# Two placements changed in a two-layer graph transformer kernel: a tile's projection copied two tiles later, and the missing-edge mask made during the experts

## The chip, the cores and the metric

The kernel runs on one core of a Trainium2 chip. A core has five engines that run side by side, each with a queue of its own: TensorE (PE, matmuls and transpositions), VectorE (DVE), ScalarE (ACT), GpSimd (POOL) and SyncE (SP, which here only starts transfers). The metric is the device time of one execution in microseconds (us). Results in matmuls stand in PSUM banks until DVE or ACT copies them to SBUF.

## What is computed

625 nodes with 512 features go through two layers. Each adds to `x` a graph network and a linear attention over the normalized rows, and then a mixture of experts. Cut to what the change touches:

```python
edge_index = jnp.stack([src, dst])
xn = layernorm(x)
x = x + rgcn(xn, edge_index, edge_type) + linear_attention(xn)   # layer 0
x = x + experts_0(layernorm(x))          # one of 8 experts for a row
xn = layernorm(x)
x = x + gat_network(xn, edge_index) + linear_attention_1(xn)     # layer 1
x = x + experts_1(layernorm(x))          # router on x @ Wg

def gat_conv(x, edge_index, W, b, a_src, a_dst, n):
    src, dst = edge_index, with a loop added for each node
    h = x @ W
    s_src, s_dst = h @ a_src, h @ a_dst
    e = leaky_relu(s_src[src] + s_dst[dst], 0.2)
    coef = softmax of e over the edges of each dst
    return segment_sum(h[src] * coef, dst) + b
# gat_network, first step: x1 = gat_conv(x, ..., W1, ...) + x @ Wsk1 + bsk1
```

The kernel does the graph attention densely: with a 625 x 625 matrix of edge counts and a mask that is -1e30 where a pair has no edge.

## The kernel before

The nodes are five tiles of 125 rows (P = 125, NT = 5). Matrices of counts (`cnt0`, `cnt1`, one for each kind of edge of layer 0) are 125 x 5 x 625 in float32 and stay in SBUF throughout.

Most of the order of instructions is the framework's: it sorts the instructions of each engine by their place in the program, their priority and what they wait for. Where `manual_schedule` is entered, the named engines take the written order instead. PE's order is written out in the whole of the part described here.

**End of layer 0's network.** The loop at L651 to L668 goes through the tiles: matmuls for the tile's own weights and for both relations, then on DVE `x += ps` (L659) and the layer norm (`layernorm`, L104 to L113); the tile before is transposed on PE in between (L125). The relations' weight matrices are mixed by DVE just before, in 58 long operations (L330). Behind this loop in the program come small constants of the expert stage: `up`, an index row that POOL's iota makes (L599) and DVE casts (L601), and `last_row` (L673, L675).

**The mask.** Then, for each tile (L712 to L716), POOL adds `cnt1` to `cnt0` (L713) and a loop to each node (L714), and DVE writes the mask over `cnt1` (L715). POOL's and DVE's queues are not written out by hand here. The result, `cnt` and `neg`, is first read by the first graph attention (L965, L973).

**The experts (L729 to L924).** DVE works out for each row a place in a sorted buffer (`slot`, L785). POOL scatters the normalized rows to that buffer in HBM by five indirect transfers (L810); SP reads them back expert by expert (`gathered`, L820). `block(i)` multiplies the rows of one expert by its first matrix, and its activation is done on ACT (L862) and DVE (L864); `rest()` multiplies by the second and writes the result out. The loop over i = 1 to 9 runs block i ahead of the rest of block i-1. Experts 0 and 1 take their rows from SBUF by a one-hot product, not from the buffer. `sf` (L893) is the place as a float, from which the last block's rows are selected. At the end POOL gathers each tile's results (`yg`, L917), and the last block's share arrives by matmuls (`held`).

**The projection stage (L1032 to L1071).** For each tile: `scaled` adds the experts' results to `x` on DVE (L1033), once for `held` and once for `yg`; `arrived` takes statistics (L1038, L1040 on DVE, the root on ACT at L1042); `normal` finishes them (L1047, L1048 on DVE) and writes the normalized row on ACT (L1049); the tile is transposed on PE (L125) and copied to `xnT` by `evac` (L72 on ACT); and four matrix products (eight matmuls in the trace) project it to 258 columns (L138): 128 of `h`, two scores, and 128 of the skip. ACT copies `h` with the scores (L1054), DVE adds the bias to the skip (L1055). The orders of PE, DVE and ACT are all written by hand. In turn t of the loop: arrival of t+1, normalization of t, transposition of t and its copy, then projection of t-1 and its two copies. Behind the stage `key(0)` projects for the linear attention, and the first graph attention begins with the row of scores (L943).

`evac` (L69 to L74) alternates between ACT and DVE by a counter, or takes ACT alone while `scalar_only` is set; the counter counts in both cases. It serves the transpositions of the attention passes, of `y1T`, and of the last router (`routed` at L1261 to L1277) later on.

PSUM has one-bank buffers in a pool of four (`ps1`, from which `one_bank()` takes) and two-bank buffers in another.

Of the kernel before, what the change touches and what calls it, by code (L numbers as in the profile page):

```python
# [8 lines left out]
F32 = mybir.dt.float32  # L9
# [4 lines left out]
OP = mybir.AluOpType  # L14
# [4 lines left out]
P = 125  # L19
NT = 5  # L20
D = 512
KD = 4
# [10 lines left out]
NEG_BIG = -1.0e30  # L33


def cols(t):
    return slice(t * P, (t + 1) * P)


def ks(k):  # L40
    return slice(k * 128, (k + 1) * 128)
# [3 lines left out]
def kernel(ctx: ExitStack, tc: tile.TileContext, A, out: bass.AP):  # L45
    nc = tc.nc
# [8 lines left out]
    xn = xv[:, :, :D]  # L55
    xnT = const.tile([128, KD, N], F32, name="xnT")
    cnt0 = const.tile([P, NT, N], F32, name="cnt0")
    cnt1 = const.tile([P, NT, N], F32, name="cnt1")
    ident = const.tile([128, 128], F32, name="ident")
# [7 lines left out]
    scalar_only = [True]  # L67

    def evac(dst, src):  # L69
        turn[0] += 1  # L70
        if scalar_only[0] or turn[0] % 2:
            nc.scalar.copy(dst, src)  # L72
        else:
            nc.vector.tensor_copy(dst, src)  # L74
# [45 lines left out]
    def transpose_rows(psum, src, dst, t, k0=0):  # L120

        n = src.shape[1] // 128
        pt = psum.tile([128, n, 128], F32, name="ps1")
        for k in range(n):
            nc.tensor.transpose(pt[:, k, :P], src[:, ks(k)], ident[:P, :P])  # L125
        evac(dst[:, k0:k0 + n, cols(t)], pt[:, :, :P])
# [9 lines left out]
    def mm(ps, pairs):  # L136
        for i, (l, r) in enumerate(pairs):
            nc.tensor.matmul(ps, l, r, start=(i == 0), stop=(i == len(pairs) - 1))  # L138
# [28 lines left out]
    def two_banks():  # L167
        return banks[0].tile([128, 2 * BANK], F32, name="ps2")

    def one_bank():  # L170
        return banks[1].tile([128, BANK], F32, name="ps1")
# [229 lines left out]
    for n in BGROUPS:  # L401
        k = BROWS * n
# [3 lines left out]
        ps = one_bank()  # L406
# [70 lines left out]
    ps1 = ctx.enter_context(tc.tile_pool(name="ps1", bufs=4, space=PSUM))  # L477
# [80 lines left out]
    sums = []  # L558
    for t in range(NT):
        ps = one_bank()  # L560
# [90 lines left out]
    for t in range(NT):  # L651
        ps = begun[t] if t in begun else one_bank()
# [17 lines left out]
    lpool2 = ctx.enter_context(tc.tile_pool(name="late2", bufs=1, side="right"))  # L670
# [18 lines left out]
    def softmax8(pool, ps, bias=None):  # L689
        lg = pool.tile([P, NT, 8], F32, name="lg")  # L690
        if bias is None:
            nc.vector.tensor_copy(lg, ps)
        else:
            nc.vector.tensor_add(lg, ps, bias)
        mx = pool.tile([P, NT], F32, name="mx")
        nc.vector.tensor_reduce(mx, lg, AX.X, OP.max)
        nc.vector.tensor_sub(lg, lg, mx[:, :, None].to_broadcast([P, NT, 8]))
        nc.scalar.activation(lg, lg, AF.Exp)
        sm = pool.tile([P, NT], F32, name="sm")
        nc.vector.tensor_reduce(sm, lg, AX.X, OP.add)  # L700
        nc.vector.reciprocal(sm, sm)
        nc.vector.tensor_mul(lg, lg, sm[:, :, None].to_broadcast([P, NT, 8]))
        return lg

    def router(pool, wr, bias=None):
# [2 lines left out]
            mm(ps[:P, 8 * t:8 * t + 8], [(xnT[:, k, cols(t)], wr[:, 8 * k:8 * k + 8]) for k in range(KD)])  # L708
        return softmax8(pool, ps[:P, :8 * NT].rearrange("p (t e) -> p t e", e=8), bias)


    for t in range(NT):  # L712
        nc.gpsimd.tensor_add(cnt0[:, t, :], cnt0[:, t, :], cnt1[:, t, :])  # L713
        nc.gpsimd.tensor_add(cnt0[:, t, cols(t)], cnt0[:, t, cols(t)], ident[:P, :P])  # L714
        nc.vector.tensor_scalar(cnt1[:, t, :], cnt0[:, t, :], 0.0, NEG_BIG, op0=OP.is_equal, op1=OP.mult)  # L715
    cnt, neg = cnt0, cnt1  # L716

    junk_pool = []

# [9 lines left out]
    with ExitStack() as st:  # L729
# [7 lines left out]
        ps = one_bank()  # L737
# [46 lines left out]
        slot = rows.tile([P, NT], I32, name="slot")  # L784
# [95 lines left out]
        def scores():  # L880
            w = w8.tile([128, KD, 258], F32, tag="w", name="wl1")
            junk_pool.append(rows)
            for i, n in ((0, "L1_gnn_W1"), (130, "L1_gnn_Wsk1")):
                nc.sync.dma_start(w[:, :, i:i + 128], A[n].rearrange("(k p) m -> p k m", p=128))
            for k in range(KD):
                for i in range(2):
                    weight_dot(w[:, k, 128 + i:129 + i], w[:, k, :128], a1[i])
            wl1.append(w)

        def last_rows():  # L890

            sf = rows.tile([P, NT], F32, name="sf")
            nc.vector.tensor_add(sf, lo, hi)  # L893
            ps = two_banks().rearrange("p (t q) -> p t q", q=128)
            for t in range(NT):
                nc.tensor.transpose(ps[:, t, :P], sf[:, t:t + 1].to_broadcast([P, 128]), ident[:P, :P])
            sel = hp.tile([128, NT, 128], F32, tag="sel", name="sel_last", bufs=NEAR)[:, :, :P]
            nc.vector.tensor_scalar(sel, ps[:, :NT, :P], last_row, None, op0=OP.is_equal)
            return sel

        rest = block(0)
        for i in range(1, 8 + SURE):
            if i == 4:
                sel_last = last_rows()
            if i == 7 + SURE:
                scores()
            after = block(i)
            rest()
            rest = after
# [21 lines left out]
    with ExitStack() as st:  # L931
# [94 lines left out]
        with ExitStack() as s1:  # L1026
# [5 lines left out]
            def scaled(t, m):  # L1032
                nc.vector.scalar_tensor_tensor(x[:, t, :], m, top[:, t:t + 1], x[:, t, :], op0=OP.mult, op1=OP.add)  # L1033

            def arrived(t):
                scaled(t, yg[t])
                st6 = small.tile([P, 6], F32, name="ln_st")
                nc.vector.bn_stats(st6, x[:, t, :])  # L1038
                mv = small.tile([P, 2], F32, name="ln_mv")
                nc.vector.bn_aggr(mv, st6)  # L1040
                sd = small.tile([P, 1], F32, name="ln_sd")
                nc.scalar.activation(sd, mv[:, 1:2], AF.Sqrt, bias=eps5[:P])  # L1042
                return mv, sd

            def normal(t, mv, sd):
                rs = small.tile([P, 2], F32, name="ln_rs2")
                nc.vector.reciprocal(rs[:, 0:1], sd)  # L1047
                nc.vector.tensor_scalar(rs[:, 1:2], mv[:, 0:1], rs[:, 0:1], -1.0, op0=OP.mult, op1=OP.mult)  # L1048
                nc.scalar.activation(xn[:, t, :], x[:, t, :], AF.Identity, scale=rs[:, 0:1], bias=rs[:, 1:2])  # L1049

            def projected(t):
                ps = one_bank()
                mm(ps[:P, :258], [(xnT[:, k, cols(t)], wl1[:, k, :]) for k in range(KD)])
                nc.scalar.copy(h1[:, t, :], ps[:P, :130])  # L1054
                nc.vector.tensor_add(sk1[:, t, :], ps[:P, 130:258], bb1)  # L1055

            scalar_only[0] = True
            with tc.manual_schedule(engines={mybir.EngineType.DVE, mybir.EngineType.Activation}):
                for t in range(NT):
                    scaled(t, held[t])  # L1060
                ahead = arrived(0)
                for t in range(NT):
                    this = ahead
                    if t < NT - 1:
                        ahead = arrived(t + 1)
                    normal(t, *this)
                    transpose_rows(ps1, xn[:, t, :], xnT, t)
                    if t:
                        projected(t - 1)
                projected(NT - 1)  # L1070
            scalar_only[0] = False  # L1071
            gather_pool.close()
            hp = s1.enter_context(tc.tile_pool(name="heads", bufs=2))
            key(0)
# [3 lines left out]
            for t in range(NT):  # L1078
                ps = one_bank()
                mm(ps[:P, :128], [(att.cT[:, j, cols(t)], h1[:, j, :128]) for j in range(NT)])  # L1080
                nc.vector.scalar_tensor_tensor(y1[:, t, :], ps[:P, :128], att.rd[:, t:t + 1], sk1[:, t, :],
                                               op0=OP.mult, op1=OP.add)
# [33 lines left out]
            behind = None  # L1116
            for h in range(16):
# [10 lines left out]
                behind = h, hm  # L1128
# [5 lines left out]
        with ExitStack() as s2:  # L1134
# [13 lines left out]
            with tc.tile_pool(name="rows2", bufs=1) as rp:  # L1148
# [5 lines left out]
                ps = one_bank()  # L1154
# [5 lines left out]
                ps = one_bank()  # L1160
# [23 lines left out]
                ps = two_banks()  # L1184
# [80 lines left out]
            for t in range(NT):  # L1265
                ps = one_bank()
                mm(ps[:P], [(att.cT[:, j, cols(t)], h3[:, j, :]) for j in range(NT)])
                nc.vector.scalar_tensor_tensor(sk3[:, t, :], ps[:P], att.rd[:, t:t + 1], sk3[:, t, :],
                                               op0=OP.mult, op1=OP.add)
# [10 lines left out]
    with ExitStack() as st:  # L1280
# [44 lines left out]
        ps = one_bank()  # L1325
# [4 lines left out]
        for i in range(2):  # L1330
            for lo, hi in ((0, 3), (3, NT)):
                ps = one_bank().rearrange("p (t q) -> p t q", q=128)
# [13 lines left out]
        ahead = [one_bank(), one_bank()]  # L1346
        for t in range(2):
            summed(ahead[t], t, range(7))
        for t in range(NT):
            if t < 2:  # L1350
                ps = ahead[t]
                summed(ps, t, [7])
            else:
                ps = one_bank()
# [48 lines left out]
```

## Time and profile before

| | us |
|---|---|
| runs, and their median | 1008.1, 1011.93, 1012.15; median 1011.93 |
| the profiled execution | 1008.68 |
| its span | 1006.9 |
| PE busy in the span | 926.3 |
| DVE busy | 513.6 |
| ACT busy | 246.9 |
| POOL busy | 155.6 |

The granted TensorE clock is 0.967 of full speed on average over the span. A busy engine counts only instructions of arithmetic; a time in the profile begins with the span. In the views, a row of the chain has the start, the length and what ran; a row of the timeline has these, the engine, the line, the operation with output and inputs, how many, and in brackets the idle time ahead of it with what ended it. The last table that is used cuts the span into windows and gives the busy time of each engine in each.

### The profile page before, as it was taken

The page shows a single profiled execution, that of the slowest core. Times are in us where ns is not written, and L with a number is a line of the kernel's source. Part 1 is how long each engine was busy: PE and PEld are TensorE (multiplying, and loading weights), DVE is VectorE, ACT ScalarE, POOL GpSimd, SP SyncE. Part 2 cuts the span into 40 slices and gives each one's busy share as a digit, 9 for nine tenths or more (in the row PEclk, how much of TensorE's full clock was granted, in tenths as well). Part 3 has the DMA queues.
Part 4 walks back from the last instruction along what each step waited for, and adds up shares of the span by engine and source line. Part 5 has one row for each costly group of instructions (what it writes and reads, how often), then busy time and mean ns, then how long its engine had stood idle before and what let it go on. Part 6 is the DMA issues. An engine that isn't in the chain of part 4 may idle for free. (4 is left out here: it accounts for less than half of the span.)

```text
span 1006.9 us, 10154 instructions
## 1 busy us (share of the span) xinstructions
PE 926.3 (92%) x3721; PEld 501.4 (50%) x3721; DVE 513.6 (51%) x941; ACT 246.9 (25%) x434; POOL 155.6 (15%) x182
## 2 busy tenths in 40 slices
PE   3899998999999999799966999999997999997997
PEld 1344455454445544587734455555553554444553
DVE  6966643079999931312242742222337654566320
ACT  0221125311113100111122633323234352311310
POOL 4111112347000940020020000000000000010410
PEclk9999997999999999799988999999999999987999
DMA  7857768977776500779740211121230204020001
GB/s 216 257 166 210 210 173 243 244 249 266 268 264 237 175 10 1 279 259 380 256 137 21 78 42 42 42 83 43 83 105 0 84 1 124 3 82 1 1 2 48
DMA packets 73076, 135.52 MB, mean 135 GB/s; under 512 B 9071, under 2 KB 11242, under 8 KB 73025
## 3 DMA queue, kind: packets, MB, share of 16 engines
q1 hardware_dynamic: 66161, 122.61, 38.8%
q0 software_dynamic: 6208, 10.97, 3.5%
q10 hardware_dynamic: 656, 1.28, 0.5%
q8 instruction: 30, 0.49, 0.2%
q14 instruction: 21, 0.17, 0.1%
HBM read 123.88 MB, written 8.85 MB: 132 GB/s over the span
## 5 line engine op out<-in xcount | busy, mean ns | idle before, releaser
L330 DVE SCALAR_TENSOR_TENSOR wmix<-basis,att,wmix 128x2048 f32<-128x2048 f32 x58 | 141.4, 2514 | 5.9 <-DMA basis<-in_L_gnn_basis_dram 5.9
L133 PE MATMUL ps<-cnt,gx 125*128 125x512 f32 (+1 forms) x320 | 88.0, 435 | 1.0 <-ACT gx L510 1.0
L226 DVE TENSOR_SCALAR os<-iota,edges,wbits 125x626 bf16<-125x626 f16 x165 | 64.2, 463 | 29.2 <-PE tail L229 29.2
L133 PE MATMUL ps<-y1T,wh 128*128 128x512 f32 (+1 forms) x256 | 74.5, 440 | 1.4 <-DVE hm L1103 1.0
L522 PE MATMUL ps<-wmix,yT 128*125 128x512 f32 x160 | 70.5, 594 | 2.3 <-DVE wmix L330 2.3
L138 PE MATMUL ps<-hm,wh 128*128 128x512 f32 (+1 forms) x256 | 71.7, 433 | 0.0
L133 PEld LDWEIGHTS ps<-cnt,gx 125*128 125x128 f32 x320 | 48.6, 190 | 42.9 <-issue 39.5
L228 PE MATMUL main<-os,odg 125*128 125x512 bf16 x165 | 52.0, 412 | 18.6 <-DVE os L226 18.6
L314 POOL DMA_DIRECT2D wmix<-stage x64 | 36.2, 568 | 157.5 <-ACT stage L311 143.6
L133 PEld LDWEIGHTS ps<-y1T,wh 128*128 128x128 f32 x256 | 41.1, 190 | 33.7 <-issue 30.6
L138 PEld LDWEIGHTS ps<-hm,wh 128*128 128x128 f32 x256 | 39.7, 191 | 30.7 <-issue 30.7
L522 PEld LDWEIGHTS ps<-wmix,yT 128*125 128x125 f32 x160 | 29.4, 188 | 37.3 <-issue 34.8
L713 POOL TENSOR_TENSOR cnt<-cnt,cnt 125x625 f32<-125x625 f32 x5 | 35.0, 7013 | 80.6 <-PE ps L133 80.6
L1113 DVE TENSOR_TENSOR acc<-acc,sg 128x625 f32<-128x625 f32 x15 | 12.2, 811 | 64.1 <-ACT sg L1111 64.1
L1103 DVE TENSOR_SCALAR hm<-ps,bh 128x625 f32<-128x625 f32 x32 | 27.7, 866 | 31.4 <-PE ps L133 31.4
L138 PEld LDWEIGHTS ps<-xgT,w1e 128*128 128x128 f32 x320 | 36.5, 192 | 7.0 <-ACT xgT L855 7.0
L138 PE MATMUL ps<-xgT,w1e 128*128 128x128 f32 x320 | 38.3, 278 | 0.7 <-ACT xgT L855 0.7
L1101 ACT ACTIVATE hm<-ps,bh 128x625 f32<-128x625 f32 x32 | 25.0, 782 | 55.0 <-PE ps L133 55.0
L125 PE MATMUL ps<-ident,xn 125*128 125x125 f32 x100 | 17.2, 303 | 22.7 <-ACT xn L1049 16.1
L228 PEld LDWEIGHTS <-odg 125*128 125x128 bf16 x165 | 17.3, 105 | 40.6 <-DVE odg L222 15.0
L133 PE MATMUL ps<-xnT,fw 128*128 128x113 f32 (+1 forms) x128 | 37.5, 455 | 0.0
L138 PE MATMUL ps<-w2e,hTe 128*128 128x512 f32 x80 | 37.4, 594 | 0.0
(332 smaller groups left out, 1425.8 us busy)
## 6 DMA issues: line engine op xcount, KB each, us to landing
basis<-in_L_gnn_basis_dram SPq DMA_DIRECT2D x128, 240.0 KB
basis<-in_L_gnn_basis_dram SPq DMA_DIRECT2D x30, 1024.0 KB
w1e<-in_L_ffn_W_dram SPq DMA_DIRECT2D x10, 1024.0 KB
w2e<-in_L_ffn_W_dram SPq DMA_DIRECT2D x10, 1024.0 KB
wh<-in_L_gnn_Wh_dram SPq DMA_DIRECT2D x4, 1024.0 KB
xd<-stage POOLq DMA_DIRECT2D x12, 256.0 KB, 3.3
b2row<-in_L_ffn_b_dram SPq DMA_DIRECT2D x10, 256.0 KB
yd<-ye POOLq DMA_DIRECT2D x9, 256.0 KB, 5.7
```

The costliest lines, as they stand in the source:

```text
L125: nc.tensor.transpose(pt[:, k, :P], src[:, ks(k)], ident[:P, :P])
L133: nc.tensor.matmul(ps[:m, lo:hi], l, r[:, lo:hi], start=(i == 0), stop=(i == len(pairs) - 1))
L138: nc.tensor.matmul(ps, l, r, start=(i == 0), stop=(i == len(pairs) - 1))
L226: nc.vector.tensor_scalar(os_, iota, edges[:, 0, c:c + 1], wfield[:, c:c + 1], op0=OP.is_equal, op1=OP.mult)
L228: nc.tensor.matmul(main0, od[:, c - c0, :], os_[:, :BANK], start=c == 0, stop=c == NE - 1)
L314: nc.gpsimd.dma_start(w[p0:p0 + 8, :, k * D:(k + 1) * D], sg[32 * j:32 * j + 16, :])
L330: nc.vector.scalar_tensor_tensor(w[:, r, :], bf, c, w[:, r, :], op0=OP.mult, op1=OP.add)
L522: nc.tensor.matmul(ps[:P], l, r, start=first and i == 0, stop=last and i == len(pairs) - 1)
L713: nc.gpsimd.tensor_add(cnt0[:, t, :], cnt0[:, t, :], cnt1[:, t, :])
L1101: nc.scalar.activation(hm[:, m, :], ps[:, :N], AF.Relu, bias=b)
L1103: nc.vector.tensor_scalar(hm[:, m, :], ps[:, :N], b, 0.0, op0=OP.add, op1=OP.max)
L1113: nc.vector.tensor_add(acc, acc, sg)
```

## The change

Two edits. The first takes the mask's loop out of its place and puts it into a function that is called at i = 3 of the expert loop, with `slot` as its argument; the mask's constant is replaced by a value read from a 125 x 1 tile that is worked out from `slot`, so that the DVE part cannot run before `slot` is there. The POOL part is the same as before and waits for no more than before.

The second splits the steps of the projection stage. The transposition (`turned`) no longer goes through `evac`; the copy to `xnT` is done on ACT as the first step of `projected`, in the next turn; and the two copies of a projection (`placed`) are a step of their own, one turn further on, so that the loop has two more turns. `scalar_only` is no longer set and reset around the stage, and `evac`'s counter is five lower afterwards than before.

```diff
-    for t in range(NT):
-        nc.gpsimd.tensor_add(cnt0[:, t, :], cnt0[:, t, :], cnt1[:, t, :])
-        nc.gpsimd.tensor_add(cnt0[:, t, cols(t)], cnt0[:, t, cols(t)], ident[:P, :P])
-        nc.vector.tensor_scalar(cnt1[:, t, :], cnt0[:, t, :], 0.0, NEG_BIG, op0=OP.is_equal, op1=OP.mult)
     cnt, neg = cnt0, cnt1
+
+    def loops_added(behind):
+
+        far = lpool2.tile([P, 1], F32, name="far")
+        nc.vector.tensor_scalar(far, behind[:, 0:1], 0.0, NEG_BIG, op0=OP.mult, op1=OP.add)
+        for t in range(NT):
+            nc.gpsimd.tensor_add(cnt0[:, t, :], cnt0[:, t, :], cnt1[:, t, :])
+            nc.gpsimd.tensor_add(cnt0[:, t, cols(t)], cnt0[:, t, cols(t)], ident[:P, :P])
+            nc.vector.tensor_scalar(cnt1[:, t, :], cnt0[:, t, :], 0.0, far, op0=OP.is_equal, op1=OP.mult)
...
         for i in range(1, 8 + SURE):
+            if i == 3:
+                loops_added(slot)
             if i == 4:
                 sel_last = last_rows()
...
-            def projected(t):
+            def turned(t):
+                pt = one_bank().rearrange("p (k q) -> p k q", q=128)
+                for k in range(KD):
+                    nc.tensor.transpose(pt[:, k, :P], xn[:, t, ks(k)], ident[:P, :P])
+                return pt
+
+            def projected(t, pt):
+                nc.scalar.copy(xnT[:, :, cols(t)], pt[:, :, :P])
                 ps = one_bank()
                 mm(ps[:P, :258], [(xnT[:, k, cols(t)], wl1[:, k, :]) for k in range(KD)])
+                return ps
+
+            def placed(t, ps):
                 nc.scalar.copy(h1[:, t, :], ps[:P, :130])
                 nc.vector.tensor_add(sk1[:, t, :], ps[:P, 130:258], bb1)
 
-            scalar_only[0] = True
             with tc.manual_schedule(engines={mybir.EngineType.DVE, mybir.EngineType.Activation}):
                 for t in range(NT):
                     scaled(t, held[t])
-                ahead = arrived(0)
-                for t in range(NT):
-                    this = ahead
-                    if t < NT - 1:
-                        ahead = arrived(t + 1)
-                    normal(t, *this)
-                    transpose_rows(ps1, xn[:, t, :], xnT, t)
-                    if t:
-                        projected(t - 1)
-                projected(NT - 1)
-            scalar_only[0] = False
+                stats, pts, sums = {0: arrived(0)}, {}, {}
+                for t in range(NT + 2):
+                    if t + 1 < NT:
+                        stats[t + 1] = arrived(t + 1)
+                    if t < NT:
+                        normal(t, *stats[t])
+                        pts[t] = turned(t)
+                    if 0 <= t - 1 < NT:
+                        sums[t - 1] = projected(t - 1, pts[t - 1])
+                    if t >= 2:
+                        placed(t - 2, sums[t - 2])
```

## The prediction

> **What bounds the kernel now.** The page's first part came first: TensorE (PE) is busy 926.3 of 1006.9 us, so time can only be saved where PE idles. The window view, cut at the changed stages, shows where (columns: window, length, busy us of PE, PE's weight loads, VectorE (DVE), ScalarE (ACT) and GpSimd (POOL), granted clock, DMA share, GB/s).
>
> ```profile
> 420.00:512.00 92.00, 87.93 (x523) 66.00 (x523) 22.87 (x86) 14.74 (x32) 10.98 (x14) 0.96 0.83 292
> 522.90:550.60 27.70, 17.32 (x60) 13.24 (x61) 5.97 (x20) 7.77 (x16) 0.53 (x5) 0.74 0.08 24
> 550.60:606.00 55.40, 53.82 (x200) 29.57 (x199) 30.47 (x86) 24.91 (x43) 0.00 (x0) 1.00 0.20 57
> ```
>
> The middle row is the projection stage: PE idles 10.4 of 27.7 us and has half its clock for part of the rest. After it PE is full for 55 us and the heads follow fuller still, so what the stage gives back moves the end one for one. The chain of waits through the stage (start, us, what) names the loop:
>
> ```profile
> 526.65 3.46 PE ps L138 x8
> 530.11 0.03 ACTq L1054
> 530.13 0.04 issue
> 530.17 0.28 ACT h L1054
> 530.45 0.04 DVEq L1055
> 530.49 0.04 issue
> 530.53 0.29 DVE sk L1055
> 530.82 0.67 DVE x L1033
> 531.49 0.02 issue
> 531.51 0.71 DVE ln_st L1038
> ...
> 532.82 0.77 ACT xn L1049
> 533.58 0.04 issue
> 533.62 0.92 PE ps L125 x4
> ```
>
> The copies of tile t-1's projection (L1054, L1055) stand ahead of tile t+1's arrival on DVE's hand-written queue; so the projection must end before the next normalization starts, and that one before the next transposition: 533.62 - 530.11 = 3.51 us with nothing on PE, then transposition and projection again. The same ring turns at 537.7 and 545.0. The view of waits agrees ("PE ps L125 <- ACT xn L1049", 16.1 us in 5 waits, one of 5.7 before the stage begins).
>
> The mask's place, in the timeline around 363 us:
>
> ```profile
> 363.47 0.24 POOL L599 IOTA up_i<- 125x128 int32 x1
> 363.74 0.23 DVE L601 CAST up<-up_i 125x128 f32<-125x128 int32 x1 [2.11 <-POOL up_i L599]
> 363.95 1.07 DVE L715 TENSOR_SCALAR cnt<-cnt 125x625 f32<-125x625 f32 x2
> 364.94 0.67 DVE L659 TENSOR_TENSOR x<-x,ps 125x512 f32<-125x512 f32 x1
> 367.72 0.65 PE L125 MATMUL ps<-ident,xn 125*128 125x125 f32 x4 [2.41 <-DVE xn L113]
> ```
>
> DVE waits 2.11 for POOL's iota, which stands behind the ten mask additions, then does two masks, then the sum L659 whose normalized tile PE waits for, 2.41 us.
>
> **The change part by part.** *Mask taken from 363 us.* The instruction order of the built kernel shows that POOL's order does not change: the additions still stand ahead of the iota, so that wait stays. Only the five DVE masks leave. Two of them (1.07, about 1.0 of own time) stood between the cast and L659. An addition beside a mask took 1.72 to 1.74 and one alone 1.50, so three of them give back some 0.7 and the iota comes that much earlier. L659 starts near 363.3 and PE's idle falls from 2.41 to 0.7: **1.7 gained** (1.0 if POOL isn't faster, 2.4 if the idle vanishes). PE is dense from there to 413.
>
> *Mask put behind `slot`.* Added: one 125x1 operation (0.2 us by its neighbours) and the same five masks, 0.47 to 0.67 each and 4.1 in all by the present group's total. They stand on DVE behind `sf` (427.6) and ahead of expert 0's first hidden copy:
>
> ```profile
> 427.87 1.28 POOL L810 DMA_INDIRECT xd<-xn,slot  x1 [63.59 <-DVE sf L893]
> 435.31 0.35 DVE L864 TENSOR_SCALAR hTe<-ps,b 128x128 f32<-128x128 f32 x1 [7.69 <-PE ps L138]
> ```
>
> DVE idles 7.69 us there, which covers them; without that cover they would cost up to 4.3. Beside them run POOL's five scatters of rows; they are priced under the rivals. I take 0.
>
> *Projection stage.* Eight matmuls took 3.46 (half clock) or 1.8 (full), four transpositions 1.09 or 0.65. In the new order DVE does tile 2's and, ahead of the sum of tile 0, tile 3's scaling; ACT does tile t+1's normalization ahead of tile t-1's copy. On paper, from the first transposition at 522.91 (kept): it ends at 524.0; tile 1's normalization is no longer behind tile 0's copy and ends at 524.8; transposition 1 to 525.9; projection 0 to 529.4; transposition 2, ready long before, to 530.5 without a gap. Projection 1 to 532.3. Transposition 3 still waits for the ring of projection 0, the same 3.51: 532.9, to 533.5. Projection 2 to 535.4. On ACT, projection 1's copy stands behind normalization 3 and its copy (533.7), so sum 534.1 and normalization 4 at 535.3: transposition 4 starts at 535.4, where it now starts at 546.80. **11.4 gained**; what follows it is the same work at the same clock. PE's order is unchanged. A sum stays in PSUM a tile longer; transpositions and sums share four banks, and the third sum takes the bank of the first one's transposition or copy, all free by 530. No queue but DVE's and ScalarE's is moved past; no transfer moves. The last copy (h of tile 4) is needed by the score row only after key(0), 3.6 us of PE.
>
> This takes the full clock from 530.2 on. Now the clock was 0.50 from 520.3 to 530.2, 1.00 to 533.9 (PE idle!), 0.50 to 537.1, 1.00 to 540.3, 0.50 to 544.0: it turns every 3.2 to 3.7 us, and always a window late. The Trainium skill ("TensorE: Matmul & The Clock Gate", "What's actually happening") says that only half and full exist, that full comes after one busy window of about 3.4 us and goes after an idle one. By the rule the denser stage keeps full speed and gains 11.4; by the durations that nearly every projection of this stage showed (3.2 to 3.5) projections 1 to 3 stay slow, the last one ends at 546.5 instead of 550.8, and 4.3 remain. I take the rule: the flips fit it.
>
> *Copies that change engine.* The transposition's copy no longer counts in the alternation between ACT and DVE; five counts less is odd, so all 31 later alternating copies swap. In the attention passes PE hardly waits for them (0.4 us in 550 to 606). In the last router PE waits 1.86, 2.26 and 0.77 for DVE's copies of tiles 0, 2, 4 and 0.67 each for ACT's of tiles 1, 3: 6.2 in all. Swapped: three by 0.67 and two between 0.77 and 2.26, 3.5 to 6.5 in all. **1.0 gained**, between 2.7 and -0.3.
>
> Sum: 1.7 + 11.4 + 1.0 = 14.1. The profiled execution took 1008.68 (span 1006.9, 1.8 around it), so 994.6; it lies 3.25 under the median of the three runs, 1011.93, which would give 997.8. The mean of the four is 1010.2, and I forecast from that: 996.1.
>
> **The rivals.**
> *The clock stays low in the stage.* For: the flips above, always late. Against: PE has hardly a gap. Then 1.7 + 4.3 + 1.0 = 7.0: 1003.
>
> *The stall only moves.* The gain of the stage is lost where transfers or DVE of the first attention pass are late. For: PE comes to key(0) 11 us earlier. Against: by the trace its weights had landed at 494, and 550 to 606 is full of PE, DVE only half busy. With half lost: 1004; with nearly all: 1009.
>
> *The mask starves the scatters: slower.* The Trainium skill ("SBUF — State Buffer", "SBUF: two separate sides") warns that while DVE runs an operation in a two-port mode POOL can't write the descriptors of its own DMAs; its figure is 620 ns grown to 3100. The masks would run exactly when POOL writes five scatters. By the page's figure 5 x 2.5 = 12.4 us late. The gathers need all scatters, and expert 2's rows come some 3.4 us before PE takes them, so 9 are lost: 1010.2 - 14.1 + 9 = 1005, still faster. By the worst row of this trace, the first mask addition, 28.3 us beside DVE's long products against 1.5 alone, 26.8 late, 23.4 lost: 1019.5. It turns slower once the scatters are over 3.4 + 14.1 = 17.5 late. Against: POOL can be held no longer than DVE works, some 4.3, of which 3.4 is slack; and the gathers of rows at 513 to 520, beside DVE's scaling, took 1.20 to 1.26 each, as the scatters do now (1.18 to 1.28). A gain has no reason here; 0 to 0.9 lost is what the rows allow, and I take 0.
>
> **How the numbers follow.** About 0.5%, 5 us, is what a measurement of this kernel can tell from no change. Chances: forecast 0.70 (990.5 to 1001: full clock a window earlier or later, worth 1.5 to 3, and the base unsure by 2); low clock 0.13 (1000 to 1006); stall moved 0.09 (most of it within 0.5%); slower 0.08. The range 990.5 to 1006 holds the first two and part of the third. Faster: 0.70 + 0.12 + 0.02 = 0.84; same 0.01 + 0.07 = 0.08; slower 0.08.
>
> **What would show it.** In the changed profile: PE without a gap before the transpositions of tiles 2 and 4 and one of about 0.6 before tile 3; the wait for `xn` in the stage down from 10.4 to 1 or 2; clock 1.00 from about 530; the stage 16 to 17 us long; the idle before transposition 0 at 366 near 0.7, with DVE still waiting for the iota; masks at 427, scatters at 1.2 each and expert 2's rows in time. I am wrong if the scatters take several us each, if the stage keeps 0.50, or if idle appears between 540 and 600 that wasn't there.

## The result and the profile after

The changed kernel took 994.18 us (median of 4 runs, 992.65 to 995.93) against 1010.36 (4 runs, 1008.1 to 1012.15): a ratio of 0.9842, 95% interval 0.9812 to 0.9872, or 16.2 us less (13 to 19). 996.1 was forecast. The profiled execution took 992.65 (span 990.8, clock 0.971).

One kernel's runs scatter: 31 runs of the kernel before, on one chip, lay between 1004.55 and 1013.64, the five fastest with a mean granted clock of 0.967 to 0.970, the five slowest with 0.957 to 0.964. So small terms are read from the traces here: PE's order is the same in both kernels, and the time from the start of one named PE instruction to the start of another can be compared between them. Many stretches repeat to 0.1 us; the ones that do not are, besides the changed places, those where the clock drops.

When it drops can be told closely. In each of the fourteen traces the granted clock is 0.50 or 1.00, and its changes within one trace lie whole multiples of 3.41 us apart: around the stage, at 530.4, 533.9, 537.3, 540.7 and 544.1 in the kernel before, and at 520.7 and 527.5 in the changed one. (A window of 1 us in which it changes gives the moment: 0.78 from 530 to 531 is 0.44 us at half clock.) So two executions of the same order can differ by whole windows of 3.41 us at half clock. The profiled pair:

| stretch, from the start of its first PE instruction | before | after | difference |
|---|---|---|---|
| start to the last relation products (351) | 351.31 | 350.91 | -0.40 |
| from there to the transposition behind the mask | 16.41 | 14.69 | -1.72 |
| layer 0's last transposition to the first of the projection stage (experts) | 109.91 | 111.38 | +1.47 |
| projection stage, up to key(0) | 27.88 | 15.63 | -12.25 |
| second graph attention (741 to 776) | 35.19 | 35.92 | +0.73 |
| last router and the first products behind it (897 to 932.7) | 35.93 | 32.33 | -3.60 |
| all the rest | | | -0.3 |

The windows of the changed kernel, cut at the projection stage and the first graph attention (columns as before):

```profile
522.30:537.90 15.60, 13.48 (x61) 11.04 (x62) 5.93 (x20) 7.40 (x16) 0.52 (x5) 0.83 0.15 43
537.90:593.30 55.40, 53.91 (x200) 29.47 (x199) 29.75 (x86) 25.51 (x43) 0.00 (x0) 1.00 0.20 57
```

The stage has the same instructions on PE, and PE now idles 2.1 of 15.6 us. In the same cut before, to the start of key(0), it was 10.4 of 27.9, so 8.3 of the gain is idle time. The other 4.0 is PE's own work done at a higher clock (17.5 us busy before, 13.5 now). The attention behind it takes 55.40 with 53.91 busy, as it did before with 53.82: nothing is given back there.

The chain of waits through the stage:

```profile
525.26 2.92 PE ps L138 x8
...
528.20 0.28 ACT h L1071
...
528.56 0.29 DVE sk L1072
...
530.85 0.76 ACT xn L1056
...
531.66 0.65 PE ps L1061 x4
532.31 1.82 PE ps L138 x8
534.13 0.43 PE ps L1061 x4
534.56 6.92 PE ps L138 x24
```

The ring is turned once instead of three times: from the projection's end at 528.18 through copy, sum, arrival and normalization to the transposition of tile 3 at 531.66, and 1.32 of that is left as idle time since projection 1 fills the rest. Behind it PE is dense.

The mask's old place, in the timeline:

```profile
362.34 0.23 POOL L599 IOTA up_i<- 125x128 int32 x1
362.61 0.23 DVE L601 CAST up<-up_i 125x128 f32<-125x128 int32 x1 [9.49 <-POOL up_i L599]
362.81 0.68 DVE L659 TENSOR_TENSOR x<-x,ps 125x512 f32<-125x512 f32 x1
365.60 0.65 PE L125 MATMUL ps<-ident,xn 125*128 125x125 f32 x4 [0.69 <-DVE xn L113]
```

DVE still waits for POOL's iota, now 9.49 us because it has no masks to make meanwhile; but what PE waits is 0.69 instead of 2.41. And the new place, beside the scatters:

```profile
425.96 2.54 DVE L720 TENSOR_SCALAR cnt<-cnt,far 125x625 f32<-125x625 f32 x5
...
426.06 1.71 POOL L815 DMA_INDIRECT xd<-xn,slot  x1 [62.92 <-DVE far L716]
428.07 1.49 POOL L815 DMA_INDIRECT xd<-xn,slot  x1 [0.30 <-issue]
```

The two scatters that run beside the masks take 1.71 and 1.49 instead of 1.28 and 1.19; the others take 1.18 to 1.19, as before. PE waits for none of it.

### The profile page after: what moved, and what is told of

The parts are those of the page before. It is cut to its first block, busy times and chain, and to the rows that moved or that the text cites. A ratio compares the mean times of both kernels' runs of the same rounds, so it can differ in the third digit from the quotient of the medians.

```text
span 990.8 us, 10155 instructions
## 1 busy us (share of the span) xinstructions
PE 921.9 (93%) x3721; PEld 499.5 (50%) x3721; DVE 512.4 (52%) x941; ACT 246.6 (25%) x435; POOL 154.2 (16%) x182
## 3 DMA queue, kind: packets, MB, share of 16 engines
q10 hardware_dynamic: 656, 1.28, 0.5%
## 5 line engine op out<-in xcount | busy, mean ns | idle before, releaser
L1129 DVE TENSOR_TENSOR acc<-acc,sg 128x625 f32<-128x625 f32 x15 | 12.2, 811 | 64.3 <-ACT sg L1127 64.3
L718 POOL TENSOR_TENSOR cnt<-cnt,cnt 125x625 f32<-125x625 f32 x5 | 32.2, 6467 | 82.6 <-PE ps L133 82.6
L229 PE MATMUL tail<-os,odg 125*128 125x114 bf16 x165 | 37.3, 226 | 0.0
L133 PE MATMUL ps<-xnT,wq 128*128 128x113 f32 (+1 forms) x128 | 36.4, 437 | 0.8 <-ACT cT L72 0.8
```

What stands on the lines that cost most here:

```text
L133: nc.tensor.matmul(ps[:m, lo:hi], l, r[:, lo:hi], start=(i == 0), stop=(i == len(pairs) - 1))
L229: nc.tensor.matmul(tail0, od[:, c - c0, :], os_[:, BANK:], start=c == 0, stop=c == NE - 1)
```

## The experiments

The theory: the projection stage waited for its own ring, in which DVE's sum of one tile stood ahead of the arrival of another; the mask is worth its 1.7 us and the swap of copying engines about one. The rivals: that the clock makes the gain (or takes it back), that the gain is not from the copies' place but from the split of the transposition, that the scatters starve, that the swap is what helps in the router. Ratios are to the kernel before, run beside each on the same chip; "stage" is the projection stage and "router" the last router, both measured as in the table above (before: 27.88 and 35.93; after: 15.63 and 32.33).

**Each part alone.** *lag_only* has the stage's new order, the mask where it was, and behind the stage:

```diff
+            turn[0] += 5
```

so that later copies stay on their engines.

> Only the projection stage's new order; the mask stays where it was and the alternation of copies is set back to what it was. Theory (the ring of copies was the cost): 11.5 to 12.5 us under the kernel before, all of it between the first and the last transposition of the stage, and the last router as slow as before (waits for DVE's copies of tiles 0, 2 and 4 near 1.9, 2.3, 0.8). Rival (the denser stage is only lucky with the clock and gives back behind): under 7 us.

Measured: 995.12, ratio 0.9833 (0.9817 to 0.9849). Stage 16.16, router 34.08. The stage alone gives 11.7 in the trace, as the theory had it; the times say 15.6, more than the trace has a place for (its own execution, 998.09, is 10.6 under that of before). The expected slow router did not come back in full: its waits for copies did, but with five windows of half clock, not six.

*mask_only* moves the mask alone.

> Only the mask moved behind slot. Theory: PE's idle before the first transposition at 366 falls from 2.4 to 0.7, but the scatters beside the masks take 0.7 longer and the clock is low when the experts begin, so 0.5 to 1.7 us under the kernel before, not clear of noise. Rival (scatters starve): slower by several us.

Measured: 1007.69, ratio 0.9957 (0.9933 to 0.9981). The stretch behind the mask is 14.69, PE's wait there 0.7: 1.72 less, exactly what the full change shows. The interval, 2 to 7 us, lies above the 0.5 to 1.7 expected. Its trace shows the 1.72 and, by one window of half clock fewer, 1.8 in the router, which the mask does not touch; other stretches are longer, and its profiled run is only 0.6 under that of the kernel before. No starving.

*swap_only* puts one more count into the alternation of the kernel before, behind the stage:

```diff
             scalar_only[0] = False
+            turn[0] += 1
```

> The kernel before with one more count in the alternation, so that every later alternating copy changes engine, nothing else. Theory: the last router gives 3 to 4 us: the first router product waits 0.7 for ScalarE's copy and not 1.9 for VectorE's, and with that gap gone the clock is not halved for the 6.8 us that follow. Rival (the clock's windows are a matter of chance and the router's gain in the one profile too): 0.5 to 1.5 us, with half clock again near 900.

Measured: 1006.51, ratio 0.9967 (0.9945 to 0.9989). The interval is 1 to 6 us less. Its router took 33.91: 2.0 less than in the profile of before, but no less than in the profiles that keep the old engines (lag_only 34.08, mask_only 34.12). PE's products in the router show why (first the kernel before, then this one, then the changed kernel, which has the same swap):

```profile
898.91 1.71 PE L138 MATMUL ps<-wg,xnT 128*125 128x8 f32 x8 [1.86 <-DVE xnT L74]
900.48 7.23 PE L138 MATMUL ps<-h,cT 125*125 125x512 f32 x10
```

```profile
897.82 1.04 PE L138 MATMUL ps<-wg,xnT 128*125 128x8 f32 x8 [0.67 <-ACT xnT L72]
898.72 4.54 PE L138 MATMUL ps<-h,cT 125*125 125x512 f32 x10
...
905.28 1.04 PE L138 MATMUL ps<-wg,xnT 128*125 128x8 f32 x8 [1.60 <-DVE xnT L74]
906.18 6.23 PE L138 MATMUL ps<-h,cT 125*125 125x512 f32 x10
```

```profile
893.00 1.04 PE L138 MATMUL ps<-wg,xnT 128*125 128x8 f32 x8 [1.61 <-DVE xnT L74]
893.89 4.54 PE L138 MATMUL ps<-h,cT 125*125 125x512 f32 x10
```

The same ten products take 4.54 at full clock, and 7.23 where the clock is 0.50 for the first 5.4 us. The swap takes the long wait from the first product and puts one of 1.60 before the second. In swap_only the clock drops behind it; in the profile of the changed kernel the same wait, 1.61, leaves it at 1.00. So the theory's 3 to 4 us are not there: the gap is moved from one tile to another, and whether the clock drops behind it is not settled by its length.

*unswapped* is the changed kernel with `turn[0] += 5` behind the stage.

> The changed kernel with five counts put back in the alternation: lag and mask without the swap of engines. Theory: the swap's 3 to 4 us are lost again, 997 to 998. Rival (swap worth little): 994 to 995.5, as the changed kernel.

Measured: 994.07, ratio 0.9821 (0.9805 to 0.9838); router 33.94. The theory falls, the rival holds: taking the swap away costs nothing that can be measured. By the medians the three parts alone give 15.6, 3.1 and 4.3 us, 23 together, where the whole gives 16.2; intervals from four or five executions promise too much for terms of this size. Of the 3.6 us that the profiled pair differ by in the router, most is one slow pass in the profile of before and one quick one in that of after.

**Halves of the stage.** *placed_late* leaves the transposition's copy behind its own normalization and moves only the two copies of a projection (shown against the changed kernel; the mask is made in its old place):

```diff
                     nc.tensor.transpose(pt[:, k, :P], xn[:, t, ks(k)], ident[:P, :P])
-                return pt
+                nc.scalar.copy(xnT[:, :, cols(t)], pt[:, :, :P])
...
-            def projected(t, pt):
-                nc.scalar.copy(xnT[:, :, cols(t)], pt[:, :, :P])
+            def projected(t):
...
                     if t >= 2:
                         placed(t - 2, sums[t - 2])
```

> Of the projection stage only the two copies of a projection are a turn later; the copy of the transposition stays right behind the normalization. Mask and alternation as before. Theory (the wait was DVE's sum standing ahead of the next arrival): this alone gives nearly all of the stage, 10.5 to 12 us under the kernel before. Rival (the transposition's copy ahead of the next normalization on ScalarE matters as well): under 8 us.

*turned_split* is the other half:

```diff
-                    if t >= 2:
-                        placed(t - 2, sums[t - 2])
+                        placed(t - 1, sums[t - 1])
```

> The other half alone: the transposition's copy goes behind the next normalization, the two copies of a projection stay in its own turn. Mask and alternation as before. Theory: no gain beyond the second transposition's 0.5 to 1 us; the gaps of about 3.5 before the transpositions of tiles 2 to 4 stay. Rival: 4 us or more.

Measured: placed_late 999.9, ratio 0.9908 (0.9877 to 0.994), stage 18.51; turned_split 1010.46, ratio 1.0012 (0.9997 to 1.0026), stage 29.92. PE's transpositions of tiles 3 and 4 in placed_late (tile 2's has no wait):

```profile
537.14 0.65 PE L1054 MATMUL ps<-ident,xn 125*128 125x125 f32 x4 [2.34 <-ACT xn L1049]
...
540.11 0.65 PE L1054 MATMUL ps<-ident,xn 125*128 125x125 f32 x4 [0.58 <-ACT xn L1049]
```

and of tiles 2 and 3 in turned_split:

```profile
535.25 0.76 PE L1054 MATMUL ps<-ident,xn 125*128 125x125 f32 x4 [3.53 <-ACT xn L1049]
...
542.79 1.09 PE L1054 MATMUL ps<-ident,xn 125*128 125x125 f32 x4 [3.43 <-ACT xn L1049]
```

The split alone keeps the full gaps, and its only effect on tile 1 (the second transposition 1.90 behind the first, not 2.65) is lost again at the end: tile 4's copy stands behind tile 3's on ScalarE (0.84 us of wait), and the clock drops once more, so that the stage ends 2.0 later than before. The late copies alone give 9.4 of the stage's 12; they need the split as well for the last 2 to 3 us, for without it ScalarE copies tile 0 before it normalizes tile 1, and the gap before tile 3 is 2.34, not 1.32. The theory said 10.5 to 12 for them and was a little high (9.1 by the medians).

**The clock.** *kept_busy* is the kernel before with the projection of tiles 0 to 3 computed twice, so that PE works on in the ring's gap; the second result is not read.

```diff
+                if t < NT - 1:
+                    spare = one_bank()
+                    mm(spare[:P, :258], [(xnT[:, k, cols(t)], wl1[:, k, :]) for k in range(KD)])
                 nc.scalar.copy(h1[:, t, :], ps[:P, :130])
```

> The kernel before with the products of tiles 0 to 3 computed a second time into a bank that nobody reads, behind each projection, where PE waits for the ring. The order is not changed. Theory (the stage loses by gaps and by the clock that follows them): the ring's links of 3.5 us stay, but clock 1.00 from the second turn makes projection and transposition 2 us shorter in each, 3 to 5 us under the kernel before. Rival (clock irrelevant, or the extra products themselves cost): 0 to 2 us slower.

Measured: 1006.54, ratio 0.9982 (0.9964 to 1.0001); stage 26.51. PE's row of sixteen products (tile 1's projection, twice) and the transposition of tile 3 behind it:

```profile
536.41 3.65 PE L138 MATMUL ps<-wl,xnT 128*125 128x258 f32 x16
541.75 0.65 PE L125 MATMUL ps<-ident,xn 125*128 125x125 f32 x4 [1.69 <-ACT xn L1049]
```

With the gap filled the clock is 1.00 from 533 on: sixteen products take 3.65, where eight took 3.36 before, and the turn from tile 2 to tile 3 (535.92 in this trace to 541.75) falls from 7.51 to 5.83. By the times the gain, 2.4 by the medians, is not clear of nothing and short of the 3 to 5 expected; the trace gives 1.4 for the stage, though the last extra product (1.8) lies on the path itself. So the clock's part is real and follows from the gaps, some 1.7 us a turn, and the order is the larger part.

**The scatters.** *masks_x4* writes the masks four times in the changed kernel:

```diff
+        for t in list(range(NT)) * 3:
+            nc.vector.tensor_scalar(cnt1[:, t, :], cnt0[:, t, :], 0.0, far, op0=OP.is_equal, op1=OP.mult)
```

> The changed kernel with the five masks written four times in a row behind slot: some 10 us of DVE in the same form beside all five scatters. Theory (a scatter beside masks takes 0.3 to 0.5 longer and no more): scatters 1.5 to 1.7 each, DVE late for expert 0's first hidden copy by 1.5 to 2, so 996 to 997. Rival (the masks lock the scatters out): scatters of 2 us and more or none before the masks end, expert 2's rows late by 5 or more, 1000 and over.

Measured: 995.19, ratio 0.986 (0.9824 to 0.9896). The scheduler put eleven of the twenty masks ahead of expert 0's first hidden copy and nine behind it, so DVE was not late (the rise over 994.2 is not clear), and 5.5 us of masks ran beside the scatters:

```profile
427.45 1.70 POOL L817 DMA_INDIRECT xd<-xn,slot  x1 [63.23 <-DVE far L716]
...
431.44 1.68 POOL L817 DMA_INDIRECT xd<-xn,slot  x1 [0.30 <-issue]
433.43 1.18 POOL L817 DMA_INDIRECT xd<-xn,slot  x1 [0.30 <-issue]
```

Each of the three scatters beside the row of masks takes 0.4 to 0.5 us longer, no matter how many masks follow; the fifth, with two more masks beside its second half, took 1.19. The rival falls as far as eleven masks can show it: nothing is locked out for the whole of DVE's work.

**What is left to gain.** *arrive_early* has each arrival a turn earlier on DVE:

```diff
-                    if t + 1 < NT:
-                        stats[t + 1] = arrived(t + 1)
...
                         pts[t] = turned(t)
+                    if t + 2 < NT:
+                        stats[t + 2] = arrived(t + 2)
```

> The changed kernel with each tile's arrival (scaling and statistics) one turn earlier on VectorE, so that the last arrival stands ahead of the first skip sum. Theory (what is left of the ring is the one gap before the transposition of tile 3, 1.3 us): that gap goes, the stage is 1.3 us shorter, 993 on the base of 994.2; not to be told from no change by the times, but by the gap in the trace. Rival: the gap moves to tile 4's transposition.

Measured: 994.19, ratio 0.9854 (0.9818 to 0.989); stage 15.54. The gap before tile 3 is gone, yet the stage is only 0.1 shorter than in the profile of after and 0.6 shorter than in its other profiles (16.15 in masks_x4): its first projection waits 0.52 for ScalarE's copy, and takes 3.80 instead of 3.12, since the clock rose 7.4 us into the stage and not 5.2 as in the profile of after. In the profiles where it rose as late without this edit (6.9 to 7.7 us in) the stage took 16.15 to 16.22, so the edit gives 0.6 of the 1.3 expected.

*router_act* sets `scalar_only` ahead of the last router.

> The changed kernel with all five copies in the last router on ScalarE. Theory: all five products wait about 0.7, and the 1.0 and 1.7 us that the swap gave back behind the first product (VectorE's copies of tiles 1 and 3 between its layer norms) go: router 1 to 3 us shorter than in the changed kernel. Rival (the tail of the router is set by VectorE's layer norms whoever copies): under 0.5 us.

Measured: 993.57, ratio 0.9831 (0.9797 to 0.9865); router 32.02, against 32.33 in the profile of after and 33.9 in swap_only and masks_x4, which copy on the same engines as after. All five products wait 0.7, but PE then waits 2.8 for a normalization by VectorE. The 1 to 3 us show in the trace against most profiles, not in the times; with equal half clock the gain is 1.0 (31.36 in *all_three* below against 32.33 in the profile of after, four windows each).

*iota_early* takes `up` and `last_row` from a memory pool that is there earlier (`lpool`), by which their iotas and casts move ahead of the additions:

> The changed kernel with the index row and the last row made before the mask additions of GpSimd, so that the sum L659 doesn't wait for GpSimd at 362. Theory: VectorE's sum of tile 0 starts some 8 us earlier and PE's remaining 0.7 us of idle before the first transposition goes, no more: 0.7 us.

Measured: 993.77, ratio 0.984 (0.9812 to 0.9869). In its profile the stretch behind the mask is 15.53, not shorter, since the products before it ran at half clock for 3.4 us; PE's wait before the transposition is gone. VectorE's sum starts at 362.01, only 0.8 earlier: it now waits for PE's products (6.73), which the expected 8 us left out. *all_three* puts the three together.

> The changed kernel with the arrivals a turn earlier, the router's copies on ScalarE, and the index rows early. Theory: the three add up, 1.3 + 1 to 3 + 0.7 under the changed kernel: 989 to 991.

Measured: 993.11 (989.37 to 993.6), ratio 0.9835 (0.9808 to 0.9863); stretch behind the mask 13.83 (0.86 less than after), stage 15.52, router 31.36. The terms of the index rows (0.86) and of the router (0.97) are in the trace, that of the arrivals only against profiles whose clock rose as late; the 989 to 991 forecast was too low for the median, and by the times it is not to be told from the changed kernel.

## Why the prediction was right

*Mask: right to a tenth.* 1.7 was forecast from 0.7 for faster additions and 1.0 for two masks; the stretch is 1.72 shorter in this kernel and in mask_only, and longer or shorter elsewhere only where the clock dropped or the iota was moved too. The five masks took 2.54 in their new place, near the low end of the 2.4 to 4.1 that were set against the cover of 7.69, and DVE waits 6.08 for the first hidden copy even so. Of the scatters' cost, taken as 0 with 0.9 as the bound, there came 0.7 of delay on POOL and no wait on PE, as the slack of 3.4 said.

*Stage: right, and a little low.* 11.4 was forecast, 12.25 came. The paper schedule, from the first transposition on, against the trace: second transposition +1.9 (measured +1.90), end of projection 0 +6.5 (+5.9), transposition 3 +10.0 (+9.4), transposition 4 +12.5 (+11.7). The 0.6 to 0.8 is one term, the clock: it rose in the middle of projection 0, at about 527.5 (5 us into the stage), and not 7.3 us in, behind projection 0, as the prediction took it. In lag_only, where it rose 7.5 us in, transposition 4 came at +12.2 and the stage gained 11.7. The idle time before transposition 3, forecast at 0.6, shifts with it: 1.32 in the profile of after, 0.75 in lag_only. In the eight profiles with the full new order the clock rose 5.2 to 7.7 us into the stage; that it rose early in the profiled one is luck, worth 0.5 of the 12.25.

```profile
527.00:528.00 1.00, 1.00 (x4) 0.77 (x4) 0.00 (x0) 0.00 (x0) 0.00 (x0) 0.75 0.35 61
528.00:529.00 1.00, 1.00 (x8) 0.93 (x7) 0.44 (x2) 0.27 (x1) 0.10 (x1) 1.00 0.28 72
```

The flips were read a little off (530.2 and 540.3 for 530.4 and 540.7; they lie 3.41 us apart, not 3.2 to 3.7). The rule of the clock gate behind this choice (the Trainium skill, "TensorE: Matmul & The Clock Gate", "What's actually happening": half or full, full after a busy window) held in the stage: windows of a microsecond show 0.50 before 527, 0.75 in the one of the rise, and 1.00 through the rest of the stage. It did not hold everywhere: in the changed kernel's router PE counts as busy without a break from 909.8 to 913.2, at half clock, and the half clock lasted to 916.6. The rival that kept the stage at half clock would have left 4.3.

*Swap: the mis-sized term.* 1.0 was taken, from the waits of the five products alone. Those waits fell within the forecast, from 6.2 to 4.4 us in all; but PE's waits for VectorE's normalizations in the same router, which the sum left out, rose from 2.1 to 3.5. What is left in the router's time is 0.1 to 0.2, as the profiles show when they are ordered by the half clock in the stretch. With four windows of 3.41 us it took 32.41 with the old engines (kept_busy) and 32.33 with the new (after). With five it took 33.94 to 34.17 with the old (lag_only, mask_only, unswapped, placed_late and turned_split) and 33.87 to 33.92 with the new (swap_only, masks_x4 and arrive_early). With six it took 35.93 with the old (before) and 35.78 with the new (iota_early). So the 3.60 of the profiled pair is luck, six windows against four, and by the times unswapped (994.07) cannot be told from the changed kernel (994.18).

*Base.* 14.1 forecast, 16.2 measured with an interval from 13 to 19. The difference is 0.9 of the stage and, in the profiled pair, the router's luck against the 1.5 that the experts took longer. That stretch varied from 109.9 to 112.1 over all kernels, with the moved mask (109.9 in iota_early) as without it (112.1 in kept_busy), so it is not the mask's doing. It is the clock again: 1.40 of the 1.47 lie before PE's first product with an expert's rows (18.43 us from the start of the stretch before, 19.83 after), where the half clock lasted four windows (414.9 to 428.5) instead of three (417.8 to 428.1). The five profiles with four windows there took 19.5 to 19.8 to that product, the nine with three 18.2 to 18.6. So in both stretches the number of windows, not the change, made most of the difference, and in this pair the two worked against each other.

*Rivals.* The stall did not move: the window behind the stage is as full as before. The slower end, starving scatters, was priced up to 26.8 us by the worst row; it is at most 0.5 for a scatter. The figure that the Trainium skill gives for such a DMA beside VectorE ("SBUF — State Buffer", "SBUF: two separate sides"), 620 ns grown to 3100, is not what this case shows, 1.19 to 1.28 grown to 1.7 at most; the measurement decides.

## What to carry to other kernels

In an order written by hand, a copy that waits for PE belongs behind the vector work on which PE's next step depends, even if that holds a PSUM bank a tile longer; the chain shows such a ring as one engine's sum followed by another tile's first step. Work out such a stage as a schedule with the row's durations, and put the clock in as a term of its own, since a gap can be paid for again in the products behind it. Where one kernel's runs scatter by more than a term is worth, compare the time between the same two PE instructions in both traces, over several profiles and with the same number of half-clock windows in the stretch, before the term is believed.

## What the runs showed of the hardware

A POOL scatter's issue beside DVE's float32 mask operations (five in 2.54 us) takes 1.33 to 1.71 instead of 1.17 to 1.29 over all profiles, and never more, while a plain addition of POOL that takes 1.50 alone took 26.3 to 28.6 us beside a row of DVE's 2.3-us products; in the kernel before it ended at 354.9, 1.4 us after the last of them. The mask with a per-row operand took 0.53 at the shortest (0.51 from start to start in its row of five), with the constant 0.47; since POOL's additions ran beside the second form only, the two are not compared like with like.

The clock changes on a grid: in each trace its changes lie whole multiples of 3.41 us apart, from the first (at 20 to 36 us) to the last. So the length of a gap does not settle whether the clock drops. A wait of 1.60 was followed by half clock from 906.7 on in swap_only, and 1.61 at the same place in the changed kernel was not; 1.85 before the stage's last transposition in the kernel before (546.8) was not either. Nor does the share of busy time alone: with PE busy for 1.56 of the 3.41 us from 544.1 in the kernel before it stayed full, with 1.81 of those from 903.3 in swap_only it fell. Stretches of identical work so differ by 1.4 to 3.6 us between profiles.
